# A two-layer transformer kernel: the batch-axis layer closes with tokens on the partitions, the router's columns stand beside its weights, and set-up of the later stages stands elsewhere

## The chip, the cores and the metric

The kernel runs on one core of a Trainium2 chip. The metric is the device time of one execution in microseconds (us). A change counts by the median of several executions, a profile is one execution. The engines are TensorE (PE, with its weight loads as PEld), VectorE (DVE), ScalarE (ACT) and GpSimd (POOL). SyncE (SP) issues most transfers. Each engine works through its own queue in order. Matrix products land in PSUM, which has eight banks of 128 x 512 float32; the rest lies in SBUF, 128 partitions wide.

## The reference

The input is `x` of 16 sequences, 512 tokens each, 128 channels, float32. Layer 0 is linear attention and a channel mix, layer 1 a retention and a small transformer block with a mixture of experts. Each part is wrapped in a modulated layer norm and a gate. The last part matters here: its attention runs over the **batch axis** (16 sequences, at one position of time), and its router sends each token to one of eight experts.

```python
def _mha(x, Wqkv, bqkv, Wo, bo):             # x: (S=16, B=512, D=128), H=4
    qkv = x @ Wqkv.T + bqkv
    q, k, v = ...                            # per head (B, H, S, hd)
    scores = einsum('bhqd,bhkd->bhqk', q, k) / sqrt(hd)
    o = einsum('bhqk,bhkd->bhqd', softmax(scores), v)
    return o.reshape(S, B, D) @ Wo.T + bo

def _moe(x, Wg, W1, b1, W2, b2):
    idx = argmax(x @ Wg.T)
    for e in range(8):
        out += (idx == e) * (relu(x @ W1[e] + b1[e]) @ W2[e] + b2[e])

y = layer_norm(h + _mha(h), g1, be1)
z = layer_norm(y + _moe(y), g2, be2)
x = x + gb * z
```

## The kernel before

**Three stages.** Stage one (`both_layers`, 0 to 797 us) takes each of the 16 sequences through layer 0 and the retention, four sequences at a time. It ends, for each, with a modulated norm that is stored to `h_rows` in DRAM (L845) and a residual that is stored to `token_rows` (L841). Stage two (`attend_and_route`, about 811 to 1049 us) takes 16 blocks of 512 tokens, each block 32 positions of time by 16 sequences, through the batch-axis attention and the router. Stage three (from 1071 us) runs 39 expert tiles, each a gather, two products with the weights of one expert, a layer norm and a scatter to the output.

**The order.** Each chain (a sequence in stage one, a block in stage two) is a Python generator. It yields a string such as `"P1.6"` or `"A1.6|V0.6"`, the cost in us that its author gives the step on each engine; a `+` marks cost that the chain itself doesn't wait for. The function `queued` keeps a planned time for each engine and always advances the chain whose planned time is the earliest. The order of these advances is the order of instructions in every queue, SP's included. Two arguments set how far apart chains start by plan, and how many may be open: `10.0, WIDTH` (4) in stage one, `11.0, 6` in stage two. A new chain starts no earlier than an old one's end once all places are taken. The numbers only order the program; on the chip each engine goes as fast as its waits allow.

**A block of stage two.** Four loads on SP's queue fetch 4 x 128 rows of `h_rows` into `rows` (L942, two buffers). PE transposes them (L946), and ACT copies them to `hb`, channels on the partitions (L948). PE makes queries and keys (L952) and values by token (L968). ACT and DVE spread the keys over heads into `k_own` (L961, L963), ACT copies the values to `vt` (L977). PE makes scores (L983), and a softmax goes through DVE (L992, L1001), POOL (L1003), ACT (L1007), DVE (L1010, L1011), POOL (L1013), DVE's transpose (L1018) and ACT's spread into `att_own` (L1022). PE multiplies with the values (L1028), ACT adds a bias (L1038), PE applies the output weights to all 512 tokens with channels on the partitions (L1041), and DVE adds the bias and the block's own input in place (L1043).

`route` then turns the sum back: PE transposes it into a bank (L1068) and makes the router's products, eight columns a token, into `few_ps` (L1071). DVE takes mean and variance from that bank (L1082, L1084), POOL the inverse root (L1087, L1088), ACT writes the normalised rows from the bank (L1095), and SP stores them (L1102). DVE finds the expert with the largest logit through small steps on 128x32 (L1107 to L1132), PE counts by products with a triangle `tri` and with `ones` (L1137, L1138), DVE makes positions (L1140 to L1165), and POOL scatters the token numbers into the list `order` (L1168, four scatters a block). All PSUM tiles of a block but `few_ps` come from seven banks in rotation.

**Around it.** Between stages one and two stand: a fill of `order`, the load of all expert weights `wex` into `ex` (4 MB, issued at L874), 64 small products that give each expert's bias through its second weights (L885, added at L892), the router's weights (`wg`, L899 to L910), `tri` and `ones`, and fills of `k_own` and `att_own` (L930, L933). Between stages two and three a chain of small DVE steps (L1197 to L1241) turns the counts into a table of slots, and two gathers fetch the lists of tokens (L1245). The tiles of these tables lie in the pool `tp`, which is opened where stage two's pools have been closed, and takes their memory.

Of the kernel before, what the change touches and what calls it, by code (L numbers as in the profile page):

```python
# [28 lines left out]
P = 128  # L29
# [5 lines left out]
NBLK = 16  # L35
# [152 lines left out]
def tile_adaln(ctx: ExitStack, tc: tile.TileContext, x, wa, wb, vec, wex, const, out):  # L188
# [202 lines left out]
    mod_sb = cp.tile([B, NMOD, C], F32, name="mod_sb")  # L391
# [439 lines left out]

    def both_layers(b):
# [12 lines left out]
        nc.sync.dma_start(out=h_rows.rearrange("(s g p) c -> s p g c", s=B, p=P)[b], in_=xn)  # L845

# [27 lines left out]
    nc.sync.dma_start(out=ex[:, :, 0 : E_NB1], in_=wex)  # L874
# [7 lines left out]
    eo = bank()  # L882
    for e in range(NE):
        for f in range(NFC):
            mm(  # L885
                eo[:, e : e + 1],
                lhsT=ex[:, e, E_W2 + f * C : E_W2 + (f + 1) * C],
                rhs=v(V_B1 + e * NFC + f),
                start=f == 0,
                stop=f == NFC - 1,  # L890
            )
    nc.vector.tensor_tensor(  # L892
        ex[:, :, E_OUT], eo[:, 0:NE], vec_sb[:, V_B2 : V_B2 + NE], ALU.add
    )

    wg = ep.tile([P, NE], F32, name="wg")
    nc.vector.tensor_scalar(wg, wcol(wb_sb, B_GATE, NE), v(V_G1), None, ALU.mult)  # L899
    wg_ps = bank()  # L900
    mm(wg_ps[:, 0:NE], lhsT=cen, rhs=wg, start=True, stop=True)
    mm(
        wg_ps[:, NE : 2 * NE],
        lhsT=v(V_BE1).to_broadcast([P, P]),
        rhs=wcol(wb_sb, B_GATE, NE),
        start=True,
        stop=True,
    )
    wgc = ep.tile([P, 2, NE], F32, name="wgc")
    nc.vector.tensor_copy(wgc.rearrange("p a e -> p (a e)"), wg_ps[:, 0 : 2 * NE])  # L910

    tri = ep.tile([P, P], BF16, name="tri")
    nc.vector.tensor_copy(tri, wcol(con, K_TRI))
    ones = ep.tile([P, P], BF16, name="ones")
    nc.gpsimd.memset(ones, 1.0)
# [7 lines left out]
    few_ps = p1.tile([P, 2, 2, P], F32, tag="few", name="few_ps", bufs=1)  # L923
# [15 lines left out]
    def attention(i, h):  # L939
        rows = work("rows")  # L940
        for g in range(4):
            nc.sync.dma_start(out=groups(rows)[:, g, :], in_=h_group[:, :, 4 * i + g, :])  # L942
        yield "D3.0"
        h_ps = bank()
        for g in range(4):
            nc.tensor.transpose(groups(h_ps)[:, g, :], groups(rows)[:, g, :], ident)  # L946
# [117 lines left out]
    def route(i, r):  # L1064
# [16 lines left out]
        for g in range(4):  # L1081
            nc.vector.bn_stats(st[:, g, :], t_ps[:, g * C : (g + 1) * C])  # L1082
# [369 lines left out]
```

## Time and profile before

| | |
|---|---|
| nine runs, median | 1281.21 us (1273.08 to 1291.05) |
| profiled execution | 1278.91 us, its span 1276.8 us |
| mean granted TensorE clock | 0.877 |
| PE busy, share of the span | 990.2 us, 78% |
| DVE | 805.4 us, 63% |
| ACT | 627.7 us, 49% |
| POOL | 565.4 us, 44% |

The span runs from the first to the last instruction of the profiled execution; the time of a run has some 2 us around it. Busy time says which engine is loaded, not what sets the end; that is read from the chain of waits, which goes back from the last instruction to whatever released it, and so on to the start. A line such as `L983` is a line of the kernel before.

### The profile page before, as it was taken

The page shows a single profiled execution, that of the slowest core. Times are in us where ns is not written, and L with a number is a line of the kernel's source. Part 1 is how long each engine was busy: PE and PEld are TensorE (multiplying, and loading weights), DVE is VectorE, ACT ScalarE, POOL GpSimd, SP SyncE. Part 2 cuts the span into 40 slices and gives each one's busy share as a digit, 9 for nine tenths or more (in the row PEclk, how much of TensorE's full clock was granted, in tenths as well). Part 3 has the DMA queues.
Part 4 walks back from the last instruction along what each step waited for, and adds up shares of the span by engine and source line. Part 5 has one row for each costly group of instructions (what it writes and reads, how often), then busy time and mean ns, then how long its engine had stood idle before and what let it go on. Part 6 is the DMA issues. An engine that isn't in the chain of part 4 may idle for free.

```text
span 1276.8 us, 37403 instructions
## 1 busy us (share of the span) xinstructions
PE 990.2 (78%) x15591; PEld 711.6 (56%) x15591; DVE 805.4 (63%) x2328; ACT 627.7 (49%) x1099; POOL 565.4 (44%) x619
## 2 busy tenths in 40 slices
PE   3888988898878698978889886876777723888883
PEld 3565555666556465655656554644455512666663
DVE  7468666756666546766767776256667732666663
ACT  0754545643555534466454553255666622555552
POOL 5114334323342422442433435224546654677774
PEclk9899988988889778988889998587879856999998
DMA  4531334411142422123342134114444222233331
GB/s 152 123 69 30 59 77 102 114 44 30 35 99 69 108 72 40 29 70 82 91 98 55 30 75 170 54 26 33 40 46 36 33 25 76 74 97 101 100 93 36
DMA packets 154634, 89.24 MB, mean 70 GB/s; under 512 B 76751, under 2 KB 142319, under 8 KB 154337
## 3 DMA queue, kind: packets, MB, share of 16 engines
q1 hardware_dynamic: 144960, 65.36, 25.3%
q0 software_dynamic: 8928, 18.24, 5.2%
q8 instruction: 123, 2.02, 0.7%
q10 hardware_dynamic: 576, 3.25, 0.7%
q14 instruction: 47, 0.38, 0.1%
HBM read 46.61 MB, written 31.22 MB: 61 GB/s over the span
## 4 chain that ended last, share of the span: by engine, by line
PE 39%; DVE 26%; POOL 12%; ACT 9%; issue 7%; DMA 6%; another core or an unknown queue 1%; POOLq 0%; SPq 0%; ACTq 0%; DVEq 0%
PE out_ps L1316 5%; PE h_ps L1302 5%; PE bank L486 4%; DVE q L428 3%; PE scores L621 3%; PE bank L605 3%; DVE hid L1312 3%; PE bank L657 3%; POOL rs L425 2%; DVE st L419 2%; DMA order<-con,idx 2%; DVE sc L625 2%; PE bank L641 2%; PE bank L699 2%; ACT kh L522 2%
## 5 line engine op out<-in xcount | busy, mean ns | idle before, releaser
L428 DVE TENSOR_SCALAR q<-x,mv,rs 128x128 f32<-128x128 f32 x256 | 87.5, 397 | 54.9 <-POOL rs L425 54.6
L522 ACT ACTIVATE kh<-k,con 128x512 f32<-128x512 f32 x128 | 83.8, 715 | 56.9 <-POOL k L788 51.4
L621 PE MATMUL scores<-ident,sc 128*128 128x128 f32 x512 | 85.5, 318 | 26.8 <-DVE sc L625 13.8
L605 PE MATMUL bank<-kh,q 32*32 32x128 f32 x4096 | 100.3, 291 | 6.5 <-ACT kh L522 1.8
L614 ACT COPY sc<-bank 128x512 f32<-128x512 f32 x128 | 68.9, 584 | 56.7 <-PE bank L605 56.1
L625 DVE TENSOR_TENSOR sc<-scores,con 128x1024 f32<-128x1024 f32 x64 | 77.7, 1213 | 29.4 <-PE scores L621 29.3
L1316 PE MATMUL out_ps<-hid,w 128*128 128x256 f32 (+1 forms) x312 | 71.5, 372 | 26.9 <-DVE hid L1312 26.8
L621 PEld LDWEIGHTS scores<-ident,sc 128*128 128x128 f32 x512 | 68.6, 163 | 42.1 <-ACT sc L614 26.5
L1349 POOL DMA_INDIRECT out_x<-z,put x71 | 71.6, 1008 | 36.0 <-issue 12.3
L605 PEld LDWEIGHTS bank<-kh,q 32*32 32x32 f32 x4096 | 72.3, 110 | 27.0 <-issue 8.3
L590 POOL COPY states<-inc 32x576 f32<-32x576 f32 x64 | 42.6, 665 | 99.0 <-DVE inc L578 95.2
L1168 POOL DMA_INDIRECT order<-con,idx x64 | 62.9, 983 | 50.4 <-issue 21.0
L657 PE MATMUL bank<-states,q 128*32 128x144 f32 x960 | 77.9, 423 | 4.5 <-issue 4.0
L1282 POOL DMA_INDIRECT x_in<-token_rows,take x71 | 70.6, 994 | 23.3 <-issue 16.5
L590 ACT COPY states<-inc 32x576 f32<-32x576 f32 x64 | 42.8, 668 | 73.5 <-DVE inc L578 72.0
L444 ACT ACTIVATE h<-bank,mod 128x512 f32<-128x512 f32 x48 | 37.2, 777 | 81.2 <-PE bank L442 81.0
L1316 PEld LDWEIGHTS out_ps<-hid,w 128*128 128x128 f32 x312 | 53.0, 190 | 39.9 <-DVE hid L1312 35.0
L1291 ACT COPY w<-ex 128x1029 f32 x39 | 40.8, 1052 | 68.4 <-DVE acc L1325 33.5
L1312 DVE TENSOR_TENSOR hid<-h_ps,w 128x1024 f32<-128x1024 f32 (+1 forms) x39 | 44.0, 1129 | 47.9 <-PE h_ps L1302 47.9
L641 PEld LDWEIGHTS bank<-v_heads,sc 128*32 128x32 f32 x4096 | 49.9, 113 | 42.6 <-issue 25.9
L641 PE MATMUL bank<-v_heads,sc 128*32 128x36 f32 x4096 | 61.6, 205 | 15.4 <-DVE sc L625 6.5
L1302 PE MATMUL h_ps<-y,w 128*128 128x256 f32 (+1 forms) x312 | 70.6, 370 | 2.9 <-ACT y L1298 2.9
(254 smaller groups left out, 2487.9 us busy)
## 6 DMA issues: line engine op xcount, KB each, us to landing
v_rows<-values SPq DMA_DIRECT2D x32, 288.0 KB
v_chunks<-values SPq DMA_DIRECT2D x128, 72.0 KB
v_heads<-v_rows SPq DMA_DIRECT2D x128, 72.0 KB
gated<-mod_rows SPq DMA_DIRECT2D x16, 448.0 KB
x<-in_x SPq DMA_DIRECT2D x16, 256.0 KB
token_rows<-gated SPq DMA_DIRECT2D x16, 256.0 KB
token_rows<-ex SPq DMA_DIRECT2D x16, 256.0 KB
h_rows<-q SPq DMA_DIRECT2D x16, 256.0 KB
```

The source lines that it names most:

```text
L428: ts(xn[:, g, :], X[b][:, g, :], mv[:, g, 0:1], rs[:, g : g + 1], ALU.subtract, ALU.mult,)
L522: nc.scalar.activation(t[:, :, n, :], k.rearrange("p (n s) -> p n s", s=CH), AF.Copy, scale=con[:, K_HEAD + n : K_HEAD + n + 1],)
L590: copy(state[rows, r], inc[rows])
L605: mm(groups(s_ps[r])[c * CH : (c + 1) * CH, n], lhsT=by_block[rows, at], rhs=kh[rows, at].rearrange("p m s -> p (m s)"), start=True, stop= ...
L621: nc.tensor.transpose(groups(st_ps[:, r])[:, n], groups(sc[:, 2 * rr + r])[:, n], ident)
L625: tt(sc[:, 2 * rr : 2 * rr + 2].rearrange("p r (n t) -> p (r n) t", t=CH), st_ps.rearrange("p r (n t) -> p (r n) t", t=CH), causal.unsquee ...
L641: mm(o_ps[a][c * CH : (c + 1) * CH, k0 : k0 + RH * HV], lhsT=groups(sc[:, r])[:, g, c * CH : (c + 1) * CH], rhs=vh[:, g * NC + c, :, r * H ...
L657: mm(o_ps[a][c * CH : (c + 1) * CH, n * NH * HV : (n + 1) * NH * HV], lhsT=q.rearrange("p (n s) -> p n s", s=CH)[:, at_chunk(ch)], rhs=sta ...
L1302: mm(h_ps[:, f, :], lhsT=w[:, E_W1 + f * P : E_W1 + (f + 1) * P], rhs=y, start=True, stop=True,)
L1312: tt(hid, h_ps, w[:, E_NB1:E_OUT].unsqueeze(2).to_broadcast([P, NFC, n]), ALU.max)
L1316: mm(o_ps, lhsT=w[:, E_W2 + f * C : E_W2 + (f + 1) * C], rhs=hid[:, f, :], start=f == 0, stop=f == NFC - 1,)
L1349: sent = nc.gpsimd.indirect_dma_start(out=out_rows, out_offset=bass.IndirectOffsetOnAxis(ap=put[:, a, s : s + 1], axis=0), in_=z[:, a], in ...
```

## The change

- **Two sets of columns.** `w_end` holds, for the value weights and for the output weights, 128 columns and beside them eight that carry the router: values times the router's weights, and output weights times the router's weights. `b_end` holds the output bias and its router part. `router_weights` makes them from the weights, as steps of the chain of batch 4 in stage one, behind its last store.
- **The block closes by token.** Loaded rows go to `res`, 136 columns a token, in seven buffers. POOL adds the bias part to them, and the eight columns of the value product to the router's place. The output product is made in four pieces of 128 tokens with tokens on the partitions, and DVE adds each half to `res`, giving the sum and the router's logits at once. The transposes L1068 and the products L1071 are gone. Statistics and normalised rows read `res` in SBUF in place of a bank.
- **One cast less.** `hot` is written as bf16 by the comparison itself.
- **Set-up moved.** The load of `wex` is issued at the start of block 4's chain. The 64 products for the expert bias stand behind stage two, their addition behind the list's gathers. The tables lie in `ep`, a pool that is opened before stage two. `mod_sb` takes a buffer of `gated` in place of its own.
- **The plan.** Blocks start 9 apart by plan, and up to 7 are open. `hb` has 3 buffers, `vt` 3.

```diff
-    mod_sb = cp.tile([B, NMOD, C], F32, name="mod_sb")
+    mod_sb = own(WIDTH - 1, [P, NMOD, C], "gated")[0:B]
...
+    def router_weights():
+        ts(wg, wcol(wb_sb, B_GATE, NE), v(V_G1), None, ALU.mult)
+        nc.vector.tensor_copy(tri, wcol(con, K_TRI))
+        yield "V0.4"
+        wg_ps = yield from bank()
+        mm(wg_ps[:, 0:NE], lhsT=cen, rhs=wg, start=True, stop=True)
...
+        yield "P0.6"
+        nc.vector.tensor_copy(wgc.rearrange("p a e -> p (a e)"), wg_ps[:, 0 : 2 * NE])
+        back(wg_ps)
+        yield "V0.2"
+        nc.vector.tensor_copy(w_end[:, 0, 0:C], wcol(wb_sb, B_O2))
+        nc.vector.tensor_copy(w_end[:, 1, 0:C], wcol(wb_sb, B_QKV + 2 * C))
+        nc.vector.tensor_copy(w_end[:, 1, C:CE], wgc[:, 0, :])
+        wo_ps, bo_ps = yield from banks(2)
+        nc.tensor.transpose(wo_ps[:, 0:C], wcol(wb_sb, B_O2), ident)
+        yield "P0.3|V0.8"
+        nc.vector.tensor_copy(wvt, wo_ps[:, 0:C])
+        yield "V0.3"
+        mm(wo_ps[:, C:CE], lhsT=wvt, rhs=wgc[:, 0, :], start=True, stop=True)
+        for at, n, rhs in ((0, C, ident), (C, NE, wgc[:, 0, :])):
+            mm(bo_ps[:, at : at + n], lhsT=v(V_BO).to_broadcast([P, P]), rhs=rhs, start=True, stop=True)
+        yield "P1.2"
+        nc.vector.tensor_copy(w_end[:, 0, C:CE], wo_ps[:, C:CE])
+        nc.vector.tensor_copy(b_end, bo_ps[:, 0:CE])
+        back(wo_ps, bo_ps)
+        yield "V0.5"
...
+        if b == WIDTH:
+            yield from router_weights()
...
-    nc.sync.dma_start(out=ex[:, :, 0 : E_NB1], in_=wex)
-    eo = bank()
-    for e in range(NE):
-        for f in range(NFC):
-            mm(eo[:, e : e + 1], ...)
-    nc.vector.tensor_tensor(ex[:, :, E_OUT], eo[:, 0:NE], vec_sb[:, V_B2 : V_B2 + NE], ALU.add)
...
+    def halves(ps):
+        return [t[:, 0 : 2 * CE].rearrange("p (g k) -> p g k", k=CE) for t in ps]
-    def attention(i, h):
-        rows = work("rows")
+    def attention(i):
+        res = wk.tile([P, 4, CE], F32, tag="res", name="res", bufs=7)
         for g in range(4):
-            nc.sync.dma_start(out=groups(rows)[:, g, :], in_=h_group[:, :, 4 * i + g, :])
+            nc.sync.dma_start(out=res[:, g, 0:C], in_=h_group[:, :, 4 * i + g, :])
...
+        h = work("hb", 3)
         nc.scalar.copy(h, h_ps)
-        yield "A0.6"
+        nc.gpsimd.tensor_tensor(
+            res[:, :, 0:C], res[:, :, 0:C], b_end[:, 0:C].unsqueeze(1).to_broadcast([P, 4, C]), ALU.add
+        )
+        yield "A0.6|+G1.1"
...
-        v_ps = bank()
+        v_ps = [bank(), bank()]
         for g in range(4):
             mm(
-                v_ps[:, g * P : (g + 1) * P],
-                lhsT=h[:, g * P : (g + 1) * P],
-                rhs=wcol(wb_sb, B_QKV + 2 * C),
+                halves(v_ps)[g // 2][:, g % 2],
+                lhsT=groups(h)[:, g],
+                rhs=w_end[:, 1],
...
-        vt = work("vt")
-        nc.scalar.copy(vt, v_ps)
+        vt = wk.tile([P, 4, CE], F32, tag="vt", name="vt", bufs=3)
+        for a, t in enumerate(halves(v_ps)):
+            nc.scalar.copy(vt[:, 2 * a : 2 * a + 2], t)
+        nc.gpsimd.tensor_tensor(
+            res[:, :, C:], vt[:, :, C:], b_end[:, C:].unsqueeze(1).to_broadcast([P, 4, NE]), ALU.add
+        )
...
-        pr_ps = bank()
-        mm(pr_ps, lhsT=wcol(wb_sb, B_O2), rhs=o, start=True, stop=True)
-        yield "P1.0"
-        stt(h, pr_ps, v(V_BO), h, ALU.add, ALU.add)
-        yield "V0.8"
+        pr_ps = [bank(), bank()]
+        for g in range(4):
+            mm(halves(pr_ps)[g // 2][:, g % 2], lhsT=groups(o)[:, g], rhs=w_end[:, 0], start=True, stop=True)
+        yield "P1.2"
+        for a, t in enumerate(halves(pr_ps)):
+            both = slice(2 * a, 2 * a + 2)
+            tt(res[:, both], t, res[:, both], ALU.add)
+        yield "V0.9"
+        return res
...
-        t_ps = bank()
-        for g in range(4):
-            nc.tensor.transpose(t_ps[:, g * P : (g + 1) * P], r[:, g * P : (g + 1) * P], ident)
-        lg = few_ps[:, i % 2, 0]
-        for g in range(4):
-            mm(lg[:, g * NE : (g + 1) * NE], lhsT=r[:, g * P : (g + 1) * P], rhs=wgc[:, 0, :], ...)
-        yield "P1.6"
...
-            nc.vector.bn_stats(st[:, g, :], t_ps[:, g * C : (g + 1) * C])
+            nc.vector.bn_stats(st[:, g, :], r[:, g, 0:C])
...
             nc.scalar.activation(
-                row[:, g * C : (g + 1) * C],
-                t_ps[:, g * C : (g + 1) * C],
+                groups(row)[:, g],
+                r[:, g, 0:C],
...
         nc.vector.tensor_tensor(
             eq,
-            lg[:, 0 : 4 * NE].rearrange("p (g e) -> p g e", e=NE),
+            r[:, :, C:],
             rs.unsqueeze(2).to_broadcast([P, 4, NE]),
...
-            eq, eq, first.unsqueeze(2).to_broadcast([P, 4, NE]), ALU.is_equal
-        )
-        hot = small([P, 4, NE], "hot", BF16)
-        nc.vector.tensor_copy(hot, eq)
+            hot, eq, first.unsqueeze(2).to_broadcast([P, 4, NE]), ALU.is_equal
+        )
...
-        nc.vector.tensor_tensor(pos, pos, eq, ALU.mult)
+        nc.vector.tensor_tensor(pos, pos, hot, ALU.mult)
...
     def attend_and_route(i):
-        h = work("hb", 6)
-        yield from attention(i, h)
-        yield from route(i, h)
+        if i == 4:
+            nc.sync.dma_start(out=ex[:, :, 0 : E_NB1], in_=wex)
+        r = yield from attention(i)
+        yield from route(i, r)
-    queued((attend_and_route(i) for i in range(NBLK)), 11.0, 6)
+    queued((attend_and_route(i) for i in range(NBLK)), 9.0, 7)
...
     def table(shape, name, dtype=F32):
-        return tp.tile(shape, dtype, name=name)
+        return ep.tile(shape, dtype, name=name)
+    eo = sp.tile([P, NE], F32, tag="eo", name="eo", bufs=1)
+    for e in range(NE):
+        for f in range(NFC):
+            mm(eo[:, e : e + 1], ...)
...
+    nc.vector.tensor_tensor(ex[:, :, E_OUT], eo[:, 0:NE], vec_sb[:, V_B2 : V_B2 + NE], ALU.add)
```

## The prediction

> **What bounds the kernel now.** I read the page's slices and shares first, then the busy time by stage, then the chain of waits around each stage border and in a steady stretch of the batch-axis layer, and last the waits of PE, DVE and SP. The change touches the stretch from 797 to 1071 us, so that is split (span piece, length, then busy us and instructions of PE, PEld, DVE, ACT, POOL, then the granted clock, the DMA share and GB/s):
>
> ```profile
> 796.90:811.30 14.40, 14.31 (x68) 14.35 (x69) 0.71 (x4) 0.00 (x0) 6.08 (x4) 0.50 0.35 110
> 811.30:1048.60 237.30, 162.08 (x1538) 113.74 (x1538) 147.48 (x515) 132.07 (x241) 115.78 (x128) 0.79 0.34 34
> 1048.60:1071.00 22.40, 0.98 (x3) 0.43 (x3) 5.12 (x30) 0.00 (x0) 4.22 (x7) 0.50 0.04 11
> ```
>
> The first piece is set-up on PE alone, the second the sixteen blocks, the third a hole in which no engine works. In the middle no engine is full (PE 68%, DVE 62%): the order decides. The borders, in the chain of waits (start, length, what):
>
> ```profile
> 796.99 13.78 PE bank L885 x64
> ...
> 811.63 0.96 PE bank L946 x4
> ```
> ```profile
> 1047.64 10.80 DMA order<-con,idx
> ...
> 1059.67 0.18 DVE count L1197
> ...
> 1063.99 0.95 POOL listed L1245
> ```
>
> At the left border the expert biases (L885) keep the first block's transposes (L946) back. At the right one the tables (L1197 to L1241) start only when the last scatter has landed. One period of the steady part reads:
>
> ```profile
> 982.38 1.05 POOL sc L1003
> ...
> 984.12 0.69 DVE tot L1010
> ...
> 985.45 0.89 DVE pos L1161
> ...
> 987.16 0.75 DVE k_own L961
> ...
> 988.23 0.76 DVE hb L1043
> 989.03 1.06 PE few_ps L1071 x8
> 990.09 1.01 PE bank L983 x32
> ```
>
> It is a loop: softmax of block i, router tail of an older block, keys of the next, closing add, router product on PE, and only then the next scores (L983), which feed the next L1003 at 993.25. PE, in order, waits for DVE's closing add before it may start scores that don't need it. Scores of six blocks start at 943.3, 955.0, 966.6, 977.5, 990.0, 1000.9, the next at 1013.4: 11.68 us a block.
>
> ```profile
> 943.30:1013.40 70.10, 55.96 (x576) 39.94 (x576) 53.31 (x191) 48.72 (x91) 40.98 (x46) 0.89 0.39 43
> ```
>
> Over six blocks that is 9.3 us of PE, 8.9 of DVE, 8.1 of ACT, 6.8 of POOL (about 8.0 with the 0.3 us between its scatters): the period is 2.3 us above the fullest engine.
>
> **Part 1, work put into the first stage** (`router_weights`, behind batch 4). DVE: L899 0.58, L913 0.51, L910 0.18, the evictions and copies 0.17 to 0.5 each (L910 below, L913 above), some 3 us in all. PE: L901 and L902 0.57 each for two at half clock, the transpose and the four new products at 0.3 to 0.6 each, some 3 us. That stage's PE is 83% busy (658 of 797 us) and DVE 66%, so gaps exist; bounds 0 and +6, I take **+3**. The planner starts batch 8 when batch 4 ends, so later batches interleave a little differently; nothing in the trace prices that, and the nine timings, 9 us either side of the median, tell what such a shift may be worth: it goes into the range.
>
> **Part 2, left border.** L885 leaves, and with it the wait for 4 MB of `wex` (issued 783.63, L885 starts 796.95: 13.3 us). The next thing late is the first block's own load: L845 issued at 800.16 is landed by 802.65, where L942 stops waiting, 2.5 us. Four issues take 2.6 us to 805.2; with 2 us for the landing the transposes start at 807.3 in place of 811.3. The `k_own` fills on POOL end at 806.4, the `att_own` fills (2 x 1.76 us on DVE, at 812.5 now) come free with the same release at 802.7 and end by 806.3. **-4** (bounds -5 and -2).
>
> **Part 3, `wex` in the middle.** The issue now stands on SP's queue just ahead of block 4's loads and, by the planner's rule, behind block 0's row stores. SP sends the loads right after it. Packet records show that stores issued after `wex` at 788.6 to 795.1 moved only once its 4096-byte packets were done, so block 4 lands some 16 us after the issue instead of 5: 11 late. Queued behind L946 of block 4 on PE are the products of blocks 1 to 3, behind the new add on POOL the softmax of block 3; the seven `res` buffers help nothing here. Between the two places on PE stand about 3.3 us (L968, L983 of block 3 and L1137), and the other engines have puts and router tails to finish. Bounds 0 (order so far behind that the load is in time) and +11; **+6**.
>
> **Part 4, the period.** Per block, by rows of the steady stretch. PE loses L1068 (0.66) and L1071 (1.0), changes L1041 (1.12) for eight passes like L968's (1.1) and adds 8 columns to L968: 9.3 to 7.8. DVE: L1043 (0.75) becomes two adds of 128x272, each near L720's 128x256 from PSUM (0.41): +0.1; one cast less: -0.2; 8.9 to 8.8. ACT: one 128x512 copy (0.58) becomes two of 272, nearest L815's 0.38 each: +0.2. POOL gains an add like L838 (128x512, 1.27) and one of 128x32 (about 0.25): with gaps 8.0 to 9.7. So POOL becomes the fullest, close to DVE. What matters more: the router product no longer exists as a step of its own, nothing on PE waits for the closing add except L1137 much later, and the loop above is cut at L1043-L1071-L983. Also no bank is held any longer from L1068 to L1095 (945.2 to 952.6 for one block), against nine bank allocations a block in place of eight. The planner's own sums per block are V 10.7, P 10.2 before, V 10.6, G 9.4, A 9.2, P 8.9 after, with starts 11 apart before and 9 after: it ran at 11.68 for 11, and the same ratio on 10.6 gives 11.3. The floor is 9.7. I take 10.6, the middle: 1.1 less for the last eight blocks, -9. In the first eight L983 starts are 13.6 apart (834.6 to 929.8 over seven); there buffers of `rows` (SP waited 38.3 us in all for L946) and starts 11 apart cost most, both eased; 12.0 there, 1.6 x 7 = -11. **-20** (bounds: 9.7 throughout, 2.0 x 8 + 3.5 x 7 = -40; +16 as in the slower rival below).
>
> A rule speaks against this part. L1161 (both inputs in SBUF) took 0.98 us in the steady stretch, against 0.14 at best, each time beside L1013 on POOL. The Trainium skill (SBUF — State Buffer, section Who interferes with whom) has a DVE instruction with two SBUF inputs contend with a GpSimd instruction that reads SBUF, the first holding the port to its end. L1107's successor reads two SBUF tensors, and POOL reads 1.5 us more a block: by the rule one more such stall, 0.8 x 15 = +12 on the sum; L1113, two SBUF inputs already, took 0.18 here, and by that row it is 0. The sum uses 0.
>
> **Part 5, right border.** The tables move to a pool that owes nothing to the blocks' buffers. Count to list is 1059.67 to 1063.99; counts are final at 1040.2, so the 4.3 us lie beside the scatter's landing, which L1245 then waits for itself: **-4.8** with the 0.5 us between landing and count (bounds -5 and -3). L885's products come here: 13.8 us at half clock from 1040.5 end at 1054, cover 5 us over; without that cover they cost up to what they outlast it. **0**. `mod_sb`'s place, the fills and `tri`, `ones` cost nothing: they lie in waits that stay.
>
> **Sum.** +3 - 4 + 6 - 20 - 4.8 = -19.8. The profiled execution took 1278.91 us (span 1276.8 and 2.1 around it), 2.3 below the median of the nine. 1278.9 - 19.8 = **1259 us**.
>
> **Rivals.** *The loop is only replaced.* POOL's in-order queue, or the nine banks, keep the period at what it is; the planner's denser order gains no time. For it: planner 10.6 against 11; against it: the cut edge. Then +3 - 4 + 6 + 0 - 4.8 = 0: 1279.
>
> *POOL takes over, with a loss.* Each block's two new adds stand in POOL's order ahead of other blocks' L1003 and L1013, one behind a load, one behind ACT's copy, and while they run they hold up DVE's two-input work. With 1.25 as now between period and fullest engine, 9.7 gives 12.1, and one stall of 0.8 more 12.9: +1.2 x 8, and +0.8 x 7 in the early half, +15, sum +15: 1294. It decides as soon as the waits on top of POOL's 9.7 us pass some 2.7 us a block (mean period over 12.4). For it: POOL is in order, serves scatter issues of 1.27 us, and the planner counts neither the second add nor the gaps; against: POOL idles 3.7 us of each period now.
>
> *The full gain.* The period falls to 10 and the early blocks to 11.5: -13 - 15, `wex` +5, sum -29: 1250 and below.
>
> **Chances.** The forecast (1250 to 1275) 0.58, full gain (under 1250) 0.12, replaced loop 0.14, loss 0.16. 0.5% of the median is 6.4 us, about what this measurement can tell: faster 0.70, same 0.14, slower 0.16. The range 1239 to 1286 takes in the replaced loop and leaves the loss and the deepest gains out; the likeliest case's own is 1250 to 1275.
>
> **What would show it.** The first block's transposes at 807; a gap on PE before block 4's transposes of 6 to 11 us; scores 10 to 11 us apart, with PE no longer waiting for the closing add; POOL over 80% busy in the steady part; the count long before the last landing and the list 0.5 us behind it. It is wrong if scores stay 11.7 or more apart, if the first stage's length moves by more than 6 us, or if the first blocks wait for loads other than block 4's.

## The result, and the profile after

The changed kernel takes **1288.7 us** (median of 10), the kernel before 1279.9 us on the same chip (31 runs): ratio 1.0083, interval 1.0054 to 1.0112. It is 0.8% slower, where 1259 us and a range of 1239 to 1286 had been predicted. Ratios here and below come from undisturbed executions and medians from all of them, so a ratio can differ from the quotient of two medians by up to 0.4%. The profiled execution of the changed kernel (1280.8 us, span 1279.0) is its fastest; the others start at 1285.9.

Lines after the change are some 30 higher: transposes L972, keys L991 and L993, scores L1017, softmax on POOL L1037 and L1047, close on DVE L1085, root on POOL L1117 and L1118, last cast L1193, scatters L1196, 64 products L1225, their addition L1291, list L1285, load of `wex` L1208. POOL's new additions are L976 and L1009.

First the stretch from the border on, by pieces (columns as in the prediction). The changed kernel, cut at its first transposes, its last block's scores, its last index cast and the first product of stage three:

```profile
798.00:809.90 11.90, 0.01 (x1) 0.04 (x1) 4.98 (x6) 0.00 (x0) 8.48 (x7) 0.50 0.43 134
809.90:1003.70 193.80, 123.77 (x1304) 89.08 (x1304) 125.92 (x404) 122.00 (x230) 113.11 (x129) 0.80 0.41 39
1003.70:1053.00 49.30, 25.67 (x200) 23.52 (x200) 20.88 (x112) 13.24 (x28) 23.87 (x28) 0.58 0.24 22
1053.00:1076.00 23.00, 1.93 (x5) 0.80 (x5) 4.32 (x29) 2.56 (x3) 9.96 (x11) 0.50 0.11 28
```

The kernel before, cut at the same two places inside stage two:

```profile
811.50:1013.40 201.90, 148.24 (x1401) 104.00 (x1401) 131.59 (x427) 121.61 (x220) 92.07 (x102) 0.83 0.36 36
1013.40:1040.80 27.40, 13.64 (x137) 9.54 (x137) 15.73 (x88) 10.45 (x22) 17.92 (x21) 0.62 0.17 27
```

PE has 24 us less to do up to the last scores (148.2 to 123.8), and that piece is 8 us shorter. The tail, from the last block's scores to its index cast, is 22 us longer. Inside the long piece the gain is all early: first transposes to the ninth block's scores fall from 118.3 to 101.6 us, the seven periods after that rise from 83.6 to 92.2.

Two waits name what is new. Waits in stage two of the changed kernel (engine, line, what it waited for, us in total, times, longest):

```profile
PE bank L1017 <- DVE k_own L991: 56.9, 14, 9.8
...
DVE r_off L1121 <- POOL r_rs L1118: 27.2, 11, 6.0
...
POOL order L1196 <- DVE idx L1193: 14.9, 1, 14.9
```

The loop that was to be cut at the closing add is replaced: PE now waits for the keys before its scores (L983 waited 10.6 us for them before), DVE for the root on POOL (15.8 before). The third line is one single wait, and DVE's timeline shows what stands in it (start, length, engine, line, operation, and in brackets the idle time before it and what ended it):

```profile
1039.52 0.18 DVE L1191 TENSOR_REDUCE to<-pos 128x4 f32<-128x32 f32 x1
1052.81 0.17 DVE L1291 TENSOR_TENSOR ex<-eo,vec_sb 128x8 f32<-128x8 f32 x1 [13.11 <-PE eo L1225]
1053.05 0.17 DVE L1193 CAST idx<-to 128x4 uint32<-128x4 f32 x1
```

PE's timeline beside it:

```profile
1038.92 13.79 PE L1225 MATMUL eo<-vec_sb,ex 128*128 128x1 f32 x64 [0.97 <-DVE count L1237]
```

The addition of the expert bias is written after the gathers of the lists, but on DVE it stands one place ahead of the last index cast. That cast, ready at 1039.7, waits for 64 products (13.79 us, at a granted clock of 0.50) that it doesn't need. **The order of the program is not the order of the queues.** The text above the prediction, which took `queued` for the order of every queue, holds for the program only; the traces show the order that each queue had in the end, not what chose it. SP's queue shows it too: the load written at block 4 is issued before the last stores of stage one:

```profile
786.00 0.62 SPq L1208 DMA_DIRECT2D ex<-in_wex  x1
...
801.59 3.63 SPq L897 DMA_DIRECT2D h_rows<-q  x2
```

### The profile page after: what moved, and what is told of

It is laid out like the page before. It is cut to its first block, busy times and chain, and to the rows that moved or that the text cites. A ratio compares the mean times of both kernels' runs of the same rounds, so it can differ in the third digit from the quotient of the medians.

```text
span 1279.0 us, 37342 instructions
## 1 busy us (share of the span) xinstructions
PE 968.4 (76%) x15502; PEld 706.2 (55%) x15502; DVE 810.4 (63%) x2334; ACT 634.7 (50%) x1117; POOL 584.4 (46%) x651
## 5 line engine op out<-in xcount | busy, mean ns | idle before, releaser
L621 PE MATMUL scores<-ident,sc 128*128 128x128 f32 x512 | 88.6, 323 | 26.7 <-ACT sc L614 13.4
L605 PE MATMUL bank<-kh,q 32*32 32x128 f32 x4096 | 95.7, 300 | 6.7 <-ACT values L499 2.8
L1359 PE MATMUL out_ps<-hid,w 128*128 128x256 f32 (+1 forms) x312 | 71.6, 372 | 28.2 <-DVE hid L1355 28.2
L605 PEld LDWEIGHTS bank<-kh,q 32*32 32x32 f32 x4096 | 69.7, 113 | 26.5 <-issue 6.2
L1196 POOL DMA_INDIRECT order<-con,idx x64 | 62.9, 983 | 40.8 <-DVE idx L1193 14.9
L1017 PE MATMUL bank<-k_own,q 128*32 128x128 f32 x512 | 26.7, 374 | 56.9 <-DVE k_own L991 56.9
```

Of the source, the lines that this page charges most:

```text
L605: mm(groups(s_ps[r])[c * CH : (c + 1) * CH, n], lhsT=by_block[rows, at], rhs=kh[rows, at].rearrange("p m s -> p (m s)"), start=True, stop= ...
L621: nc.tensor.transpose(groups(st_ps[:, r])[:, n], groups(sc[:, 2 * rr + r])[:, n], ident)
L1359: mm(o_ps, lhsT=w[:, E_W2 + f * C : E_W2 + (f + 1) * C], rhs=hid[:, f, :], start=f == 0, stop=f == NFC - 1,)
```

## The experiments

Pieces in us, read from each run's trace in the same way, for the versions that the text compares (`T` is the first transposes, `S` the last block's scores, `idx` the last cast, `put` the last scatter issue, `list` the first gather of the lists, L1285):

| | last store | store to T | T to S | S to idx | idx to put | put to list | list to end |
|---|---|---|---|---|---|---|---|
| before | 800.2 | 11.3 | 201.9 | 27.4 | 6.8 | 16.4 | 212.8 |
| changed | 804.9 | 5.0 | 193.8 | 49.3 | 4.3 | 8.5 | 213.2 |
| e6 | 804.3 | 5.1 | 194.6 | 37.5 | 5.5 | 9.7 | 215.7 |
| e16 | 801.3 | 5.1 | 183.1 | 43.2 | 4.2 | 9.2 | 214.4 |
| e15 | 803.4 | 5.2 | 182.5 | 42.8 | 4.3 | 10.2 | 215.3 |
| e11 | 801.4 | 11.3 | 202.8 | 28.4 | 7.5 | 12.5 | 214.4 |
| e12 | 802.7 | 5.1 | 201.0 | 28.1 | 5.6 | 8.6 | 213.4 |
| e13 | 806.6 | 5.1 | 200.0 | 30.4 | 4.3 | 7.8 | 214.3 |
| e17 | 803.7 | 5.0 | 154.7 | 28.2 | 0.5 | 4.5 | 258.3 |

### The expert bias off DVE's queue (e1, e5, e6)

```diff
-    nc.vector.tensor_tensor(ex[:, :, E_OUT], eo[:, 0:NE], vec_sb[:, V_B2 : V_B2 + NE], ALU.add)
+    for e in range(NE):
+        nc.scalar.activation(ex[:, e, E_OUT:E_END], eo[:, e : e + 1], AF.Identity,
+                             bias=vec_sb[:, V_B2 + e : V_B2 + e + 1])
```

> The changed kernel, with the addition of the expert bias (L1291) taken off DVE's queue: eight small ACT instructions write the same column, so nothing on DVE waits for the 64 products. Theory A (the addition stands in DVE's queue just ahead of the last block's cast to indices, so the last four scatters wait some 13 us for PE): the last cast comes at about 1040 us in place of 1053, and the time falls by 10 to 13 us against the changed kernel, to 1275 to 1279 where the kernel before has 1280. Theory B (the batch layer itself is longer and the wait for the products lies beside other work): less than 4 us, still slower than before by 0.4% or more.

> The changed kernel as it is, beside the next ones on the same chip, since the chips differ: on the chip of e1 to e4 the kernel before took 1350 us in place of 1280, most of the difference in the expert stage. From the first result it should stand at 1.005 to 1.011 of the kernel before, with the last cast to indices 49 us behind the last block's scores.

> e1_add_on_act again, beside the changed kernel. Theory A of e1 (the addition in DVE's queue costs what PE needs for the 64 products): 10 to 13 us below e5_changed_again, the last cast 36 us behind the last scores in place of 49. Theory B: within 4 us of e5_changed_again.

The run e1 fell on a chip where the kernel before takes 1350.4 us: 1331.1, ratio 0.9853 (0.9797 to 0.9910). On another chip, e5 and e6 side by side: the changed kernel again 1.0091 (1.0054 to 1.0127), with the addition on ACT 0.9986 (0.9951 to 1.0021), 10 us less by the medians (1285.9 and 1275.7), as theory A had it. The tail fell from 49.3 to 37.5. DVE's timeline of e6 at the place of the wait:

```profile
1040.80 0.18 DVE L1191 TENSOR_REDUCE to<-pos 128x4 f32<-128x32 f32 x1
1040.92 0.69 DVE L1248 TENSOR_REDUCE pairs<-fill 128x16 f32<-128x512 f32 x1
1041.53 0.16 DVE L1193 CAST idx<-to 128x4 uint32<-128x4 f32 x1
```

One instruction in the wrong queue cost all that the changed kernel lost against the one before. The gain that was forecast is still missing.

### The tables alone, the set-up place, the plan (e2, e3, e4)

e2 is the kernel before with the tables in the pool `ep`; e3 is e1 with the old plan of 11.0 and six; e4 is e1 with the router's set-up written between the stages.

```diff
-        return tp.tile(shape, dtype, name=name)
+        return ep.tile(shape, dtype, name=name)
...
-    queued((attend_and_route(i) for i in range(NBLK)), 9.0, 7)
+    queued((attend_and_route(i) for i in range(NBLK)), 11.0, 6)
```

> The kernel before, with the slot tables alone moved to the other pool. My sum had -4.8 us for this. On DVE three steps of the tables (1.55 us together) now stand ahead of the last cast to indices, so the last scatters should come 1.5 us later: -3 us net, list gathers 0.5 us behind the last landing. If the landing itself is set by the scatters' end and the tables were not on the path, 0; if the steps ahead of the cast cost more than the tables gain, above 0.

> As e1_add_on_act, with the batch layer's plan of before: starts 11 apart, six blocks open. Theory C (the denser plan bunches two blocks' scatters on POOL, eight in a row in front of another block's softmax, and stacks the last blocks): same time as e1_add_on_act or up to 8 us less, with the second half of the blocks at 12 us a block in place of 13.2. Theory D (the denser plan is what gained time in the first half, 11.45 us a block in place of 13.6): 6 to 12 us more than e1_add_on_act.

> As e1_add_on_act, with the router's set-up out of the first stage and between the stages, where it stood before. Theory E (the extra steps behind batch 4 lengthen the first stage, whose last store of the norm is issued at 804.9 in place of 800.2 us): that store comes 3 to 6 us earlier, the set-up hides under the first blocks' loads, and the time is 2 to 5 us below e1_add_on_act. Theory F (the 4.7 us are the spread between executions): the last store within 2 us of e1_add_on_act's and the time within 2 us.

All on the chip of e1: e2 0.9971 (0.9931 to 1.0011), no difference that shows; e3 0.9946 (0.9914 to 0.9977), 0.9% above e1, about as theory D had it; e4 0.9778 (0.9717 to 0.9838), 0.8% below e1, where theory E had 2 to 5 us. In e2 three table steps, `pairs` among them, stood on DVE ahead of the last cast. So the dense plan is worth having with the new close, and the set-up inside stage one seems to cost something, though the intervals of e1 and e4 overlap.

### The keys' false order (e7)

A block's four key writes go to separate rows of one tile, two from ACT and two from DVE. Nothing says that they are separate, so each waits for the one before it across two engines.

```diff
-                ts(ko[rows, :, n], src, vec_sb[rows, V_BK : V_BK + 1], None, ALU.add)
+                put = ts(ko[rows, :, n], src, vec_sb[rows, V_BK : V_BK + 1], None, ALU.add)
...
+            apart(f"keys{i}", put.ins)
```

> As e6, with the four writes of a block's keys (two on ACT, two on DVE, each to 32 partitions of its own) declared free of each other, so that ACT's second no longer waits for DVE's first. Theory G (PE's 57 us of waiting for k_own in the changed kernel come from this chain through two queues): that wait falls to under 30 us and the time by 5 to 12 us against e6. Theory H (DVE reaches the keys late because its queue stands behind POOL's inverse root and softmax steps, and the chain itself adds little): PE's wait stays above 40 us and the time within 3 us of e6.

1271.7 us, ratio 0.9995 (0.9953 to 1.0036), against 1275.7 us and 0.9986 for e6: less by the median, not by the ratio, so no gain of the whole kernel is shown. The 56 us of waits on the keys are gone from the top of the list, and others have taken their place. Waits of e7 in stage two:

```profile
PE few_ps L1166 <- DVE hot L1159: 33.5, 6, 12.6
DVE r_off L1122 <- POOL r_rs L1119: 29.3, 11, 9.5
ACT sc L1042 <- POOL sc L1038: 24.7, 6, 10.3
```

The late half fell from 92.9 to 84.2 us, the tail rose from 37.5 to 42.7. All three waits lead back to POOL's queue: `hot` waits for the root, the root and the softmax for POOL. The declaration also changed the order of the queues: near the end of the long piece POOL has scatters in rows of 4, 1 and 3 in e6 and 8 in a row in e7. So the pieces price the two together.

### POOL's new additions (e8, e10, e18)

e8 (from e6) and e10 (from e7) replace both new POOL additions by a one-row product on PE and copies on ACT; e8 also changed the planner's costs, e10 not. e18 (from e15 below) leaves the larger addition out altogether.

```diff
-        nc.gpsimd.tensor_tensor(
-            res[:, :, 0:C], res[:, :, 0:C], b_end[:, 0:C].unsqueeze(1).to_broadcast([P, 4, C]), ALU.add
-        )
...
+            mm(halves(pr_ps)[g // 2][:, g % 2], lhsT=one_row, rhs=b_end[0:1, :], start=False, stop=True)
```

> As e6, with POOL's two additions a block gone: the bias comes through four more products of one row on PE (about 1.1 us a block), and ACT copies the router's eight columns from the bank. Theory H/I (POOL's in-order queue is what the second half of the blocks waits for; POOL serves 1.5 us less a block): 5 to 15 us below e6, the seven periods of the second half 1 us shorter each. Rival (POOL's queue isn't the limit, the work on PE and ACT counts): 0 to 8 us more than e6.

> The version with the addition on ACT and the key writes independent, minus both new POOL additions of the close: the bias of the residual and the router's columns is added by a product of one row on PE, the columns are copied on ACT; the step costs handed to the planner are left as they were, unlike in the earlier run of this idea. Nothing is left out. Theory H (POOL's queue, longer by some 22 us of work in the stage, is what holds the late half and the tail back): the stage from first transposes to last index cast falls from 228.7 us to 215 or less, and the kernel to about 1262, ratio 0.985 to 0.992. Rival I (POOL's additions lie in slack; the chain through DVE, ACT and POOL of each block sets the pace): the stage stays at 225 to 235 us and the ratio at 0.997 to 1.006, since PE gets four small products more and ACT two copies more a block.

> The version with all three edits without the addition of the closing bias to the 128 residual channels on POOL, the larger of the two POOL additions the change brought (128x512, one a block); the bias itself is left out of the result, nothing takes its place, and the order of all other work stays the same. Theory H in its clean form (POOL's new addition sets back what is queued behind it): first transposes to last index cast falls from 225.3 us by 8 or more, to 217 or less. Rival I (it lies in slack): 222 to 228 us.

e8 1.0125 (1.0082 to 1.0167), e10 1.0141 (1.0098 to 1.0185): both worse. T to idx of e10 is 253.9 us, though POOL has less to do. In both the built order of the queues changed throughout, with ten scatters in a row on POOL near the end of e10, so they show only that fewer POOL instructions don't help by themselves. e18 keeps the order; its ratio, from two executions, is 0.9821 (0.9598 to 1.0045). From T to idx it took 242.0 us, more than both expectations, on one of the slower chips (below). Up to the ninth block's scores it took 88.7 us in place of 96.6 in e15. Its late half (104.8) holds waits for which the profile names no work of this core. Waits of e18 in stage two:

```profile
ACT o L1057 <- remote: 28.0, 3, 12.9
...
DVE sc L1012 <- remote: 15.4, 4, 6.6
```

A single profile with such waits doesn't give the addition's price; what the early half shows is a hint of some 8 us, and the rest stays open.

### Plan, borders and close, one at a time (e11, e12, e13)

e11 is the kernel before with the dense plan (9.0, seven, and seven `hb`). e12 is the kernel before with only the two borders changed: products behind stage two, addition on ACT, tables in `ep`. e13 is e15 below, thinned to 10.5 and five.

```diff
-    queued((attend_and_route(i) for i in range(NBLK)), 11.0, 6)
+    queued((attend_and_route(i) for i in range(NBLK)), 9.0, 7)
...
-    queued((attend_and_route(i) for i in range(NBLK)), 9.0, 7)
+    queued((attend_and_route(i) for i in range(NBLK)), 10.5, 5)
```

> The kernel before with only the order of the batch-axis layer made as dense as in the changed kernel: starts 9.0 apart and seven blocks in flight, for 11.0 and six. Nothing is left out. Theory D (what shortened the early half and lengthened the late half and the tail is the dense order, and the token-side close by itself moves little): first transposes to eighth block's scores 100 to 108 us in place of 118.3, eighth to last 88 to 97 in place of 83.6, last scores to last index cast 33 to 42 in place of 27.4; whole kernel within 0.5% of before (ratio 0.995 to 1.005). Rival E (the close makes the dense order possible: with the closing add still ahead of PE's scores, the old loop stays): early half 113 or more, or the late half above 97, and the whole kernel slower by over 0.5%.

> The kernel before with only the two borders of the changed kernel: the 64 expert-bias products behind the batch-axis layer with their addition on ACT, and the tables in the pool that owes nothing to the blocks' buffers. The close over channels, the residual and the plan stay as before; the router's weights stay between the stages. Nothing is left out. Theory L (the borders are worth what they measured in the changed kernel, 6 us on the left and 7 on the right, and the close adds nothing to that): about 1264 us, ratio 0.987 to 0.993, last store to first transposes 5 to 7 us, last scatter to list 8 to 10 us. Rival M (what is gained at the borders is given back: the products outlast the scatter's landing at half clock, or table steps enter DVE's queue ahead of the last blocks as in the run with the tables alone): ratio 0.996 to 1.003, last scores to last index cast 30 us or more in place of 27.4.

> The version with all three edits (addition on ACT, key writes independent, router's weights folded between the stages), its blocks 10.5 apart and five in flight in place of 9.0 and seven. In this order POOL's queue never has more than four scatter issues of a late block without other work between them; in the order of 9.0 and seven it has nine, seven and six in a row at the end. Nothing is left out. Theory N (scatter issues clumped on POOL hold up the softmax and the router tails of other blocks, and so make the late half and the tail long): last scores to last index cast 27 to 32 us in place of 41.6, first transposes to last index cast 222 us or less in place of 225.2, kernel 3 to 8 us faster than the version at 9.0 and seven of the same call. Rival P (the clumps only follow the other waits; a sparser start only moves time back into the early half): first transposes to last index cast 226 to 234 us, kernel within 3 us of the other or slower.

e11 1.0066 (1.0034 to 1.0099): with the old close the dense plan moves 11 us out of the early half (118.3 to 107.3), puts 12 into the late one (95.5), and leaves the tail alone. Early and late half are as theory D had them, the tail and the total are not: the total is as rival E had it. With the new close the same step does something else: from e3 to e1, on a slower chip, the early half falls from 114.8 to 112.2 and the late one from 108.1 to 97.7. So plan and close don't add, and the halves can't be put down to either alone. e12 0.9941 (0.9905 to 0.9976), between the two expectations: the borders alone gain 0.6%; in the table they are 6.2 us shorter at the left and 7.8 between the last scatter and the list. e13 0.9935 (0.9896 to 0.9975), against 0.9853 for e15 on the same chip: the tail fell to 30.4 as one theory had it, but T to S rose to 200.0, and the sum from T to idx is 230.4 against 225.3. Spreading the starts, and with them the rows of scatters, only moves the time.

### Set-up between the stages, and the best version (e9, e15, e16, e14)

e9 and e15 are one kernel: addition on ACT, keys apart, and `router_weights` written between the stages. e16 is e7 again, beside e15. e14 is the kernel before with only the set-up moved into stage one.

```diff
-        if b == WIDTH:
-            yield from router_weights()
```

> The changed kernel with three edits together: the expert-bias addition on ACT, the four key writes of a block declared independent, and the router's folded weights (router_weights) computed between the stages instead of inside the first one. Nothing is left out. Theory J (the set-up work inside the first stage costs what Part 1 forecast, or more): against the version without the third edit (1271.7 us, ratio 0.9995 to before) this is 3 to 8 us faster, near 1265, ratio 0.990 to 0.996; its last h_rows store is issued at 800 to 804 us, as in the kernel before, and the first transposes follow by about 5 us, or by up to 9 where the set-up between the stages shows. Rival K (the first stage's ends of 803 to 812 us are spread between executions, and the set-up is hidden in both places): ratio 0.998 to 1.002, and the last store is again somewhere from 803 to 812 us.

> The version with all three edits once more, as the base of the run with 10.5 and five and of the next. Ratio 0.983 to 0.991 as in its first run; last h_rows store 794 to 803 us.

> The version with the addition on ACT and the key writes independent once more, router's weights inside the first stage, now on the same chip as the version that has them between the stages: their difference is the price of Part 1. Theory J: 5 to 13 us slower than that version, last h_rows store 803 to 812 us, ratio to before 0.994 to 1.002. Rival K: within 3 us of that version.

> The kernel before with only Part 1 of the change: the router's folded weights, tri and ones and the two operand tables of the close computed inside the first stage behind batch 4, mod_sb in the place of a buffer that is not in use yet. The two operand tables are computed but not used here; nothing else differs. Theory J (the set-up inside the first stage delays its end): the last h_rows store at 803 to 812 us in place of 800 to 803, kernel 3 to 10 us slower than before less the 2 to 3 us that the shorter piece at the left border gives back, ratio 1.001 to 1.006. Rival K (hidden): last store 799 to 803 us, ratio 0.996 to 1.000.

e9 1253.8 us against 1271.8, ratio 0.9860 (0.9806 to 0.9914); e15 0.9853 (0.9801 to 0.9906). This version **beats both kernels by over 1%**, on two chips. e16 0.9917 (0.9884 to 0.9950), so the place of the set-up is worth 0.6% in this pair, 0.8% in e1 and e4. e14, alone on the old kernel, 1.0005 (0.9969 to 1.0042): nothing that shows. The direction is the same wherever the changed close is there; the size isn't settled.

### Three scatters of four left out (e17)

```diff
-            put = nc.gpsimd.indirect_dma_start(
+            if g == 0:
+                put = nc.gpsimd.indirect_dma_start(
```

> The version with all three edits, but of each block's four scatters of token numbers only the first is issued: 48 of the 64 scatter issues on POOL, 1.27 us each, are left out, and with them three quarters of the token numbers, so that only the stage's length is read, not the experts' results. The order of all that stays is the same. Theory R (scatter issues on POOL, and the router steps and softmax steps queued behind them, set the stage's length): first transposes to last index cast falls from 225.3 us to 212 or less, last scores to last index cast to 31 or less in place of 42. Rival S (the scatters lie in waits that other steps cause): 219 us or more, tail 36 or more.

The question was what holds T to idx at 225 to 232 us in nearly every version (before 229.3, e6 232.1, e11 231.2, e12 229.1, e13 230.4, e15 225.3), whatever PE has to do. POOL's timeline in the tail of e15:

```profile
1022.50 0.96 POOL L1185 DMA_INDIRECT order<-con,idx  x1 [0.30 <-issue]
1023.76 0.96 POOL L1185 DMA_INDIRECT order<-con,idx  x1 [0.30 <-issue]
1025.02 0.96 POOL L1185 DMA_INDIRECT order<-con,idx  x1 [0.30 <-issue]
1026.29 0.96 POOL L1185 DMA_INDIRECT order<-con,idx  x1 [0.30 <-issue]
1027.27 0.21 POOL L1106 TENSOR_TENSOR r_rs<-r_mv,eps 128x4 f32<-128x4 f32 x1
...
1028.66 1.05 POOL L1107 TENSOR_TENSOR r_rs<-r_rs,power 128x4 f32<-128x4 f32 x1
```

And DVE beside it:

```profile
1019.94 0.36 DVE L1103 BATCH_NORM_AGGREGATE r_mv<-r_st 128x2 f32<-128x6 f32 x4
1029.75 0.16 DVE L1110 SCALAR_TENSOR_TENSOR r_off<-r_mv,r_rs 128x4 f32<-128x4 f32 x1 [9.45 <-POOL r_rs L1107]
```

The last block's variance is ready at 1020.3, but its root stands on POOL behind nine scatter issues in a row, 1.26 us each. In e17 POOL's and ACT's queues keep their order, DVE's too but for a few steps of the router at one place; only those issues, and the transfers that they start, are missing. Pieces T to S and S to idx of e15, then of e17:

```profile
808.60:991.10 182.50, 122.46 (x1305) 84.69 (x1309) 126.97 (x405) 120.66 (x227) 110.42 (x127) 0.83 0.37 41
991.10:1033.90 42.80, 14.20 (x149) 11.93 (x139) 21.48 (x111) 14.55 (x31) 25.74 (x31) 0.58 0.12 24
```
```profile
808.70:963.40 154.70, 110.01 (x1304) 77.32 (x1304) 123.06 (x405) 119.39 (x226) 80.94 (x96) 0.91 0.19 48
963.40:991.60 28.20, 15.17 (x143) 12.94 (x143) 21.38 (x111) 15.29 (x32) 12.14 (x16) 0.56 0.15 37
```

48 issues of some 1.27 us less are 61 us of POOL's time; the stage gives back 42 of them (225.3 to 182.9), though POOL was busy for only 136 of 225 us. DVE and ACT do nearly the same work in 42 us less. The mean period of the scores falls from 11.6 to 9.7 us. So the scatters set the pace of the stage, in the new order at least. One wait of each run, e15 then e17:

```profile
DVE r_off L1110 <- POOL r_rs L1107: 26.2, 9, 9.4
```
```profile
DVE r_off L1110 <- POOL r_rs L1107: 10.3, 10, 2.2
```

All waits of DVE and ACT for POOL's root and softmax fall together from 63.1 to 21.4 us; the two largest waits for loaded rows stay at 30.3 and 30.4. That speaks for the issues in POOL's queue. But the scatters' transfers are gone too: in the rows above the DMA share falls from 0.37 to 0.19 and the granted clock rises from 0.83 to 0.91, and SP's waits for earlier row stores fall from 38.1 us to 0.8. How much of the 42 us is owed to the transfers was not separated. The two runs also lie on different chips; e17's is one of the slower ones, on which e18 took 242.0 us, so 42 is rather too small than too large. e17's own time (1253.3 us, 1355.2 for the kernel before on that chip) tells nothing more, since its stage three works from lists that lack three quarters of the tokens.

## Why the prediction was wrong, by its own steps

**Part 1 (+3, bounds 0 and +6).** Eight profiles with the set-up inside stage one have the last store at 801.3 to 812.0 us, mean 805.4; six without it (chips with similar times only) at 794.6 to 806.6, mean 801.5. That is 3.9 us later: right, as far as so wide a spread can tell. The ratios make it more (8 to 10 us in e15/e16 and e1/e4) or nothing (e14). In the pair e15/e16 the store itself came no earlier between the stages (803.4 in e15, 801.3 in e16), so a later store is not what separates those two.

**Part 2 (-4).** Right and larger: store to transposes 11.3 to 5.0, -6.3.

**Part 3 (+6).** Failed, by its premise. The load was to stand behind block 0's row stores and delay block 4; it was issued at 786.0, ahead of stage one's last stores, and no block waited for it: 0. The trace before had shown this, in a number the prediction itself used: L874, written behind the whole of stage one, was issued at 783.63, 16 us ahead of that stage's last store.

```profile
783.63 0.62 SPq L874 DMA_DIRECT2D ex<-in_wex  x1
...
800.16 0.36 SPq L845 DMA_DIRECT2D h_rows<-q  x1
```

**Part 4 (-20).** Failed: from the first transposes to the last cast e6, which has no expert bias in the way, took 232.1 us, the kernel before 229.3, so +2.8 in place of -20. PE doesn't wait for the closing add any more, and the early half gained 16.7 us (forecast 11). But e11 gained 11.0 there with the plan alone, on the old close, so the early gain doesn't show that the cut loop was worth it. The late half lost 8.6 where 9 were to be gained, and the tail lost 10 even without the expert bias (27.4 to 37.5 in e6). The step that failed is the count of POOL, "with gaps 8.0 to 9.7", used as a floor beside other engines' loads. (Its terms, 8.0 + 1.27 + 0.25, make 9.5, and the middle of 9.7 and 11.3 is 10.5; neither matters.) Its 5.1 us of scatters a block were taken for work that fits in anywhere. Root and softmax of other blocks stand behind them in POOL's queue (9.45 us in one wait of e15), and with three of four left out the stage is 42 us shorter and the mean period is 9.7 us, the floor that had been reckoned with all four in (e17). How much of that is the issues and how much their transfers, and what POOL's new additions cost, stays open. A second miss may be the keys' order across DVE and ACT: from e6 to e7 the late half fell by 8.7 us and the tail rose by 5.2, with the queues' order changed as well.

The rule weighed there was the one on DVE and GpSimd contending for a port (the Trainium skill, SBUF — State Buffer, section Who interferes with whom). It was feared for the successor of L1107, which is L1137; here it is with the step behind it (duration in ns, shortest/median/longest):

```profile
L1137 DVE TENSOR_TENSOR eq<-res,r_rs x16: 174/184/1108, 843.7 to 1036.2; 128x32 f32<-128x32 f32 x16
L1143 DVE TENSOR_TENSOR eq<-eq,wgc x16: 143/192/1699, 843.9 to 1036.4; 128x32 f32<-128x32 f32 x16
```

Each was slow twice in sixteen, up to 1.70 us, each time beside L1037 or L1047 on POOL; before, none of the two was. Means of 286 and 332 ns against 184 and 179 add 4.1 us over the stage. L1161's successor (L1189) gave back 4.8: it was slow once, L1161 seven times. Over the six two-input steps of 128x32 in a block's router the sum is 24.9 us before and 24.6 after, so the 0 that was taken was close and +12 was not. The rows agree with the rule: each time that one of these steps took over 0.4 us, nine times before and eight after, it ran beside a softmax step on POOL.

**Part 5 (-4.8, and 0 for the products).** Right for the tables: the list stands right behind the last landing, which gains some 5 us that lay between the two before. The piece from the last scatter to the list fell by 7.9; the rest is an earlier landing, and over the eleven profiles with the new tables on chips with similar times the piece runs from 7.8 to 12.3 us. The **0 for L885's products** is the step that turned the sign. Their cover, the scatter's landing, was there, and the price without it was named, but their consumer on DVE was not followed into its queue. It stood ahead of the last index cast, so the products came before the scatter and not beside its landing: +12 in the tail, 10 us of the kernel (e5 and e6).

**Sum.** With what the profiles show: +4.7 - 6.3 + 0 - 8.1 (T to S) + 21.9 (tail) - 2.5 - 7.9 (idx to put, put to list) + 0.4 = +2.2, the difference of the spans (1276.8 and 1279.0). The medians differ by 8.8; the median of the changed kernel lies 8 us above its profiled execution, and no piece shows where the difference sits.

**Rivals.** The slower one came nearest by its number (1294). Its place, POOL, was right, its mechanism not shown: it put the loss on the new additions, and the runs that took these away gave nothing (e8, e10) or can't be read to the end (e18). What decided against the forecast was the addition on DVE. "The loop is only replaced" describes T to idx in e6 (232.1 against 229.3) well.

## What to carry to other kernels

Follow every moved instruction's consumers into their own queues, and look in the trace for an instruction that is issued before others written ahead of it: where there is one, the program's order does not tell the queue's. Here an engine that was busy for 60% of a stage set its pace: each scatter took POOL's queue for 1.27 us, and what stood behind it waited, whichever block it belonged to. Leaving scatters out shortened the stage (e17), spreading them didn't (e13). PE had 24 us less to do, and even with the addition off DVE's queue (e6) the stage kept its length; the longest waits led to other engines.

## What the hardware showed beyond that

- **Chips differ, most of all in one stage.** On one chip the kernel before took 1350 us for 1277 on another, and stage three from its first product to the end took 247 to 258 us in place of 203. Stage one was the same within its spread, stage two some 14 us longer (T to idx 246.4 in e1, 232.1 in e6, the same kernel). Stage three is the one of gathers and scatters; its best slices moved 93 to 101 GB/s in the changed kernel's profile, 72 to 84 in e18's.
- **Executions differ with the granted clock.** Over 25 executions of the kernel before on one chip, the mean clock went from 0.862 to 0.882 and the time from 1283 to 1265 us (correlation -0.89).
- **The set-up inside stage one may go with a lower clock.** From 640 to 795 us the ten profiles that have it there show a granted clock of 0.87 to 0.90, mean 0.880, the ten others 0.885 to 0.946, mean 0.914. The ranges overlap, and the pair e1 (0.904, inside) and e4 (0.885, between) goes the other way. Why was not tried.
